# A grouped 3x3 convolution behind a group normalisation: the order of vector and scalar work between images, and 16-bit integers in the weights' quantisation

## The chip, the core and the metric

The kernel runs on one core of a Trainium2 chip. Five engines work side by side and wait for each other through semaphores: PE (TensorE, matmuls), DVE (VectorE), ACT (ScalarE), POOL (GpSimd) and SP (SyncE, which issues DMAs here). Each runs its instructions in the order in which the program hands them over. The metric is the time of one execution on the device, in microseconds (us); less is better.

## The reference, cut to what matters

The input x holds 160 images of 128 channels and 32 x 32 pixels. Each is normalised over groups of four channels. A 3x3 convolution with 128 output channels follows, with one of five weight sets for 32 images each, and the result is added to x. The weights are quantised in two steps by divisions rounded down:

```python
s1 = (jnp.max(U) - jnp.min(U)) / 3.0
v1 = s1 * floor(U / s1)
s2 = s1 / 5.0
v2 = s2 * floor((U - v1) / s2)
w = (v1 + v2).reshape(OUT_CH * N, IN_CH, 3, 3)      # N = 5 sets
act = conv(x_normalised, w, groups=5, padding=1)
return x + act
```

## The kernel before

**One image at a time.** An image is a tile of 128 channels by 1024 pixels. PE multiplies fp16 numbers, so the normalised image z (L491, ACT) is split in a high part hi (L499, ACT) and a rest lo (L548, DVE, `low_part`). Of the rest only sums and differences of rows are used (rows, L561 to L564, DVE, `combinations`). `conv` gives PE the products of an image: eo, and m for products with sums and differences of pairs of rows. m leaves PSUM by a copy on ACT (mm or mw, L672, `leave`), DVE makes pq of it (L684, L685, `pairs`) and adds eo to it (sum, L707 or L705, `residual`). POOL then issues a DMA that adds the sum to x in place (L720, `accumulate`), and SP stores the image.

**Combined images.** From image 14 on, every third image (i % 3 == 2) is a combined one: DVE forms row differences and sums v of x itself (L524, L527, L530, with two edges on POOL, L520 and L521, `combine`), ACT scales them to vh (L535), DVE makes the rest vl (L541, `low_combined`).

**Buffers.** eo has two buffers, so that conv of image i + 1 needs the sum of image i - 1. m has one, so that its next products need the copy of the last.

**Statistics.** The sum and sum of squares of an image come from two ACT passes (L192, L199, `measure` with stages 0 and 1), for some early images from DVE (L182 to L186; `by_vector` says which). For a group of eight images `means` is a small matmul over channels on PE (L208), `deviations` copies its result to ngm on ACT (L217) and forms dv on POOL (L219 to L222), `variances` is a second matmul (L225), `deviation` and `scales` make the factors: ve on ACT (L231), then rstd, shift and twice on POOL. Means and variances are placed after the first third of conv's products of an image and of the next one.

**Weights.** Set 0 is quantised at the start. Each other set is quantised while the set before it is in use, a column of the 3x3 window at a time: `make_column` is a generator of 14 DVE steps for a column (nearest integer L101, floor division L110 to L114, the rest L125, again, and L446). After them come three PE transposes (L451), two copies on ACT (wt, L456 and L457) and three operations on POOL (outer, L459, and wt, L460 and L461). From the fourth image of a set on, the loop takes two steps an image. The 15th step of a set falls to image 11 of it, the 29th to image 18, the end to image 25.

**The order.** It is written out by hand in `run`: an iteration hands over conv of image i, then statistics of images some 14 ahead, the copy of m, z and hi of image i + 3 or i + 4, DVE's work, deviations and factors, late statistics, the weight steps, and loads and stores.

Of the kernel before, what the change touches and what calls it, by code (L numbers as in the profile page):

```python
# [9 lines left out]
I32 = mybir.dt.int32  # L10
MM = mybir.dt.float16
ALU = mybir.AluOpType
# [4 lines left out]
N_SETS = 5  # L17
# [17 lines left out]
class Steps:  # L35
# [56 lines left out]
            nc.vector.scalar_tensor_tensor(far, self.s2, limit, far, op, ALU.max)  # L92
        nc.vector.tensor_copy(self.far, far)

    def nearest(self, pool, v, parts, name, by_scalar=False):

        tag = "ns" if by_scalar else "nn"
        dt = mybir.dt.int16 if by_scalar else I32
        n = pool.tile(list(v.shape), dt, tag=tag, name=f"{tag}_{name}")
        engine = self.nc.scalar.mul if by_scalar else self.nc.vector.tensor_scalar_mul  # L100
        engine(n, v, parts[0])  # L101
        return n

    def floor_div(self, k, v, n, t, parts):

        nc = self.nc
        r, _, hi, lo = parts
        yield nc.vector.scalar_tensor_tensor(t, n, hi, v, ALU.mult, ALU.add)  # L110
        yield nc.vector.scalar_tensor_tensor(t, n, lo, t, ALU.mult, ALU.add)
        yield nc.vector.scalar_tensor_tensor(t, t, r, n, ALU.mult, ALU.add)
        yield nc.vector.tensor_tensor(t, t, n, ALU.is_lt)
        yield nc.vector.tensor_sub(k, n, t)  # L114

    def quantise(self, pool, un, name, dt, by_scalar=False):


        yield (nn := self.nearest(pool, un, self.parts1, name, by_scalar))
        tt, k1, k2, rest = (  # L120
            pool.tile(list(un.shape), kind, tag=tag, name=f"{tag}_{name}")
            for tag, kind in (("tt", F32), ("k1", dt), ("k2", dt), ("rest", F32))
        )
        yield from self.floor_div(k1, un, nn, tt, self.parts1)
        yield self.nc.vector.scalar_tensor_tensor(  # L125
            rest, k1, self.parts1[1], un, ALU.mult, ALU.add
        )
        yield (nn := self.nearest(pool, rest, self.parts2, name + "_2"))
        yield from self.floor_div(k2, rest, nn, tt, self.parts2)
        return k1, k2  # L130


def run(steps):

    while True:
        try:
            next(steps)
        except StopIteration as end:
            return end.value
# [169 lines left out]
class Main:  # L309
# [153 lines left out]


    def by_vector(self, i):
        return self.EARLY <= i < self.EARLY + 18 and i % 2 == 0

    def measure(self, i, stages=(0, 1)):

# [259 lines left out]
    def run(self):  # L729
        nc, P = self.nc, self.P  # L730
# [3 lines left out]
        for n in range(N_SETS):  # L734
            if n == 0:
                un = self.upool.tile([P, P, TAPS], F32, tag="u", name="u0")
# [32 lines left out]
        def take(steps, count):  # L769
            for _ in range(count):  # L770
                next(steps, None)
# [71 lines left out]
        for i in range(self.imgs):  # L843
            n, b = self.place(i)
# [29 lines left out]
                and k - 3 - (self.combined(k - 1) and self.group_of[k] == self.group_of[k - 1])  # L874
                == i
            ]
            if self.combined(i + 1):
                self.low_combined(i + 1)
            if self.combined(i + 2):
                self.combine(i + 2)  # L880

            stages = (0, 1) if self.combined(i - 1) else (0,)
            for k in to_measure:
                if not self.by_vector(k):
                    self.measure(k, stages)
            if i >= self.FIRST and not self.combined(i):
                self.leave(i)
            for k in parted:
                self.normalise(k)
            if self.combined(i):  # L890
                self.leave(i)
            for k in parted:
                self.high_part(k)
            if self.combined(i + 2):
                self.high_combined(i + 2)
            if i + 2 < self.STEADY:
                if self.FIRST < i + 2:
                    self.low_part(i + 2)
                    self.combinations(i + 2)
            if i > self.FIRST:  # L900
                self.residual(i - 1)
                self.accumulate(i - 1)

            if i >= self.FIRST and not self.combined(i):
                self.pairs(i)
            if self.STEADY <= i + 2 < self.imgs and not self.combined(i + 2):
                self.low_part(i + 2)
                self.combinations(i + 2)
            if self.combined(i):
                self.pairs(i)  # L910
            for st in middle:
                st.deviation()
                st.scales()
            for st in ready:
                st.deviations()
            middle, ready = ready, []
            for k in to_measure:
                if self.by_vector(k) or 1 not in stages:
                    self.measure(k, (1,))
                group = self.group_of[k]  # L920
                if k + 1 == self.groups[group].stop:
                    ready.append(self.stats[group])
            if b == self.per_set // 16 and n + 1 < N_SETS:
                self.load_set(n + 1)
            if b == self.per_set // 8 and n + 1 < N_SETS:
                later = (s for col in self.COLS for s in self.make_column(n + 1, col))
            if later is not None:
                take(later, 2)
                if b == self.per_set - 1:
                    run(later)  # L930
            self.store(i - 2)
            while loaded * NB < min(self.imgs, i + self.LOAD_LEAD):
                self.load(loaded)
# [50 lines left out]
```

## Time and profile before

| what | us |
|---|---|
| median of three runs | 1059.19 |
| lowest and highest | 1054.25, 1059.98 |
| profiled execution, as timed | 1059.3 |
| span of its instructions | 1057.4 |
| ACT busy | 845.8 (80%) |
| POOL busy | 400.7 (38%) |

The profiled execution was taken at a mean PE clock of 0.992. Its page gives each engine's busy time. PE's busy time says little by itself, since matmuls overlap: one of 496 columns counts as 0.38 us and the next one starts about 0.216 us later. Where PE shows idle time, it waited for something. The view of waits says for what, and the windows give the same numbers for stretches of the span. These are DVE's quantisation steps in it, each of 384 elements a partition:

```profile
L113 DVE TENSOR_TENSOR tt<-tt,nn 128x384 f32<-128x384 f32 x28 | 15.5, 555 | 0.5
L114 DVE TENSOR_TENSOR k<-nn,tt 128x384 f16<-128x384 int32 x28 | 15.5, 555 | 0.7
L446 DVE SCALAR_TENSOR_TENSOR m<-k,k 128x384 f16<-128x384 f16 x12 | 6.7, 558 | 0.4
```

The columns are line, engine, operation, output and inputs, shapes and count, then the time of all in us, the mean of one in ns, and the engine's idle time before them.

### The profile page before, as it was taken

How to read it: one execution, taken by the hardware profiler on the slowest of the kernel's cores; microseconds unless marked ns; L12 is line 12 of the kernel's file. 1: busy time of each engine (PE TensorE's matmuls, PEld its weight loads, DVE VectorE, ACT ScalarE, POOL GpSimd, SP SyncE). 2: the span in 40 equal slices, each digit the busy share in tenths (PEclk: the TensorE clock that was granted, in tenths of full speed). 3: DMA queues.
4: the chain of work that ended last, by engine and by line, in shares of the span. 5: the costliest groups of instructions: out<-in, count | busy, mean ns of one | idle time of the engine just before them, and what ended most of it. 6: DMA issues, size and time to landing. Idle time of an engine off the chain costs nothing.

```text
span 1057.4 us, 15888 instructions
## 1 busy us (share of the span) xinstructions
PE 1000.4 (95%) x5910; PEld 578.2 (55%) x5910; DVE 970.3 (92%) x1399; ACT 845.8 (80%) x1113; POOL 400.7 (38%) x517
## 2 busy tenths in 40 slices
PE   1899998999999999999999999999989999999997
PEld 0355554555565555656555555555545556565554
DVE  7999999998999999989999988899999988888975
ACT  4787696898888978988887879888969988886551
POOL 4432426272325253442445262525242623333410
PEclk9999998999999999999999999999999999999999
DMA  9548988899998998999899898998989999988673
GB/s 362 209 132 207 239 239 239 229 243 263 280 264 255 236 253 224 272 279 270 247 244 250 235 284 240 274 241 240 247 233 249 256 275 263 260 213 213 159 179 123
DMA packets 67286, 254.42 MB, mean 241 GB/s; under 512 B 5248, under 2 KB 5248, under 8 KB 67200
## 3 DMA queue, kind: packets, MB, share of 16 engines
q1 hardware_dynamic: 45168, 173.09, 47.8%
q0 software_dynamic: 22032, 80.23, 39.3%
q8 instruction: 48, 0.79, 0.3%
q14 instruction: 38, 0.31, 0.1%
HBM read 89.19 MB, written 83.89 MB: 164 GB/s over the span
## 4 chain that ended last, share of the span: by engine, by line
PE 44%; DVE 40%; issue 7%; POOL 5%; ACT 3%; DMA 1%; SPq 0%; POOLq 0%; DVEq 0%; ACTq 0%
PE eo L588 20%; PE m L624 12%; PE eo L624 11%; DVE sum L707 5%; DVE lo L548 5%; DVE vl L541 4%; DVE rows L561 3%; DVE v L524 2%; DVE sum L705 2%; DVE rows L563 2%; DVE rows L564 2%; DVE pq L684 1%; DVE pq L685 1%; DVE v L527 1%; ACT vh L535 1%
## 5 line engine op out<-in xcount | busy, mean ns | idle before, releaser
L588 PE MATMUL eo<-hi,wt 128*128 128x496 f16 (+3 forms) x1998 | 483.7, 379 | 4.5 <-DVE sum L705 2.4
L624 PEld LDWEIGHTS <-wt 128*128 128x128 f16 x3690 | 361.7, 99 | 218.2 <-issue 3.3
L720 POOL DMA_DIRECT2D xt<-sum x153 | 134.6, 880 | 547.6 <-DVE sum L707 291.4
L588 PEld LDWEIGHTS <-wt 128*128 128x128 f16 x2070 | 204.1, 99 | 202.7 <-issue 12.7
L624 PE MATMUL eo<-rows,wt 128*128 128x248 f16 (+1 forms) x1308 | 198.1, 274 | 0.0
L199 ACT ACTIVATE junk<-xt,mv 128x1024 f16<-128x1024 f32 x151 | 173.2, 1147 | 1.6
L192 ACT ACTIVATE junk<-xt 128x1024 f16<-128x1024 f32 x151 | 159.1, 1054 | 13.7 <-DMA xt<-in_x_dram 10.9
L672 ACT ACTIVATE mm<-m 128x1024 f16<-128x1024 f32 x109 | 110.8, 1017 | 66.2 <-PE m L624 64.9
L624 PE MATMUL m<-rows,wt 128*128 128x496 f16 (+1 forms) x654 | 159.1, 379 | 0.8 <-ACT mm L672 0.6
L541 DVE SCALAR_TENSOR_TENSOR vl<-v,rstd,vh 128x2048 f16<-128x2048 f32 x48 | 112.8, 2349 | 34.0 <-ACT vh L535 34.0
L491 ACT ACTIVATE z<-xt,shift,rstd 128x1024 f32<-128x1024 f32 x112 | 137.8, 1230 | 5.3 <-POOL shift L241 5.3
L548 DVE TENSOR_TENSOR lo<-z,hi 128x1024 f16<-128x1024 f32 x112 | 137.0, 1223 | 0.0
L535 ACT ACTIVATE vh<-v,rstd 128x2048 f16<-128x2048 f32 x48 | 95.9, 1999 | 50.8 <-DVE v L530 36.4
L707 DVE SCALAR_TENSOR_TENSOR sum<-pq,eo 128x1024 f32<-128x1024 f16 x105 | 127.6, 1215 | 7.6 <-PE eo L624 7.6
L499 ACT CAST hi<-z 128x1024 f16<-128x1024 f32 x112 | 116.7, 1042 | 2.2
L624 PE MATMUL eo<-vl,wt 128*128 128x248 f16 (+1 forms) x576 | 110.2, 273 | 0.0
L624 PE MATMUL eo<-vh,wt 128*128 128x248 f16 (+1 forms) x576 | 110.1, 273 | 0.0
L624 PE MATMUL m<-vl,wt 128*128 128x496 f16 (+1 forms) x288 | 109.3, 380 | 0.0
L624 PE MATMUL m<-vh,wt 128*128 128x496 f16 (+1 forms) x288 | 109.3, 380 | 0.0
L672 ACT ACTIVATE mw<-m 128x1024 f32<-128x1024 f32 x48 | 48.7, 1015 | 48.7 <-PE m L624 48.6
L561 DVE TENSOR_TENSOR rows<-lo 128x1024 f16<-128x1024 f16 x109 | 75.9, 696 | 3.7
L684 DVE TENSOR_TENSOR pq<-mm 128x512 f16<-128x512 f16 x109 | 45.9, 421 | 18.8 <-ACT mm L672 18.8
(114 smaller groups left out, 990.2 us busy)
## 6 DMA issues: line engine op xcount, KB each, us to landing
xt<-in_x_dram SPq DMA_DIRECT2D x78, 1024.0 KB, 9.4
out_dram<-xt SPq DMA_DIRECT2D x78, 1024.0 KB, 5.5
xt<-sum POOLq DMA_DIRECT2D x153, 512.0 KB, 6.8
range<-in_L_conv_U_dram SPq DMA_DIRECT2D x4, 576.0 KB, 7.1
u<-in_L_conv_U_dram SPq DMA_DIRECT2D x4, 576.0 KB, 12.1
xt<-in_x_dram SPq DMA_DIRECT2D x4, 512.0 KB, 9.3
out_dram<-xt SPq DMA_DIRECT2D x3, 512.0 KB, 2.8
u<-in_L_conv_U_dram SPq DMA_DIRECT2D x2, 288.0 KB, 2.9
```

Source lines behind the costliest of these rows:

```text
L192: self.nc.scalar.activation(junk, image, ACTF.Copy, scale=-1.0 / image.shape[1], accum_out=self.mv[:, j, 0:1],)
L199: self.nc.scalar.activation(junk, image, ACTF.Square, bias=self.mv[:, j, 0:1], accum_out=self.mv[:, j, 1:2],)
L491: nc.scalar.activation(z, self.image(i), ACTF.Identity, bias=st.shift[:, j : j + 1], scale=st.rstd[:, j : j + 1],)
L499: self.nc.scalar.copy(hi.rearrange("p h w -> p (h w)"), self.z[i])
L541: self.nc.vector.scalar_tensor_tensor(vl, self.v[i], st.rstd[:, j], self.hi[i], ALU.mult, ALU.subtract)
L548: self.nc.vector.tensor_sub(lo[:, 1 : self.H + 1, :].rearrange("p h w -> p (h w)"), self.z.pop(i), self.hi[i].rearrange("p h w -> p (h w)"),)
L561: nc.vector.tensor_sub(d, lo[:, 0:H, :], lo[:, 2 : H + 2, :])
L588: nc.tensor.matmul(target[:, h, r0 - h0 : r1 - h0, c0:c1], self.wts[n, col][:, k, :], tile[:, s0 : s0 + r1 - r0, c0 + dw : c1 + dw], start ...
L624: nc.tensor.matmul(target[:, :, c0:c1], self.wts[n, col][:, kind, :], source[:, :, c0 + dw : c1 + dw], start=start, stop=stop,)
L672: self.nc.scalar.mul(m, self.m.pop(i).rearrange("p a i w -> p a (i w)"), scale)
L707: nc.vector.scalar_tensor_tensor(self.sum[i], self.m.pop(i), 0.5 / UP, eo, ALU.mult, ALU.add)
L720: self.nc.gpsimd.dma_start(self.image(i), self.sum.pop(i), accum_op=ALU.add)
```

## The change

In the quantisation the nearest integers become int16 and the result of the comparison becomes fp16 (`below`), so that the last subtraction has 16-bit operands alone. In the loop DVE's and ACT's operations are put in another order, in which one that reads a result seldom follows the one that wrote it; the weight steps move from the end of the iteration to places before and after `pairs`, ahead of the deviations; and fewer images have their statistics from DVE (four in place of nine).

```diff
-    def nearest(self, pool, v, parts, name, by_scalar=False):
+    def nearest(self, pool, v, parts, name, dt, by_scalar=False):
...
-        yield nc.vector.tensor_tensor(t, t, n, ALU.is_lt)
-        yield nc.vector.tensor_sub(k, n, t)
+        yield nc.vector.tensor_tensor(below, t, n, ALU.is_lt)
+        yield nc.vector.tensor_sub(k, n, below)
...
+        ints = mybir.dt.int16 if dt == MM else I32
+        yield (nn := self.nearest(pool, un, self.parts1, name, ints, by_scalar))
...
+        below = pool.tile(list(un.shape), MM, tag="lt", name=f"lt_{name}") if dt == MM else tt
...
-        return self.EARLY <= i < self.EARLY + 18 and i % 2 == 0
+        return self.EARLY <= i < self.EARLY + 8 and i % 2 == 0
...
-            if self.combined(i + 1):
-                self.low_combined(i + 1)
-            if self.combined(i + 2):
-                self.combine(i + 2)
-
-            stages = (0, 1) if self.combined(i - 1) else (0,)
-            for k in to_measure:
-                if not self.by_vector(k):
-                    self.measure(k, stages)
+            if b == self.per_set // 16 and n + 1 < N_SETS:
+                self.load_set(n + 1)
+            if b == self.per_set // 8 and n + 1 < N_SETS:
+                later = (s for col in self.COLS for s in self.make_column(n + 1, col))
+            by_scalar = [k for k in to_measure if not self.by_vector(k)]
+            for k in by_scalar:
+                self.measure(k, (0,))
+            if self.combined(i - 1):
+                for k in by_scalar:
+                    self.measure(k, (1,))
             if i >= self.FIRST and not self.combined(i):
                 self.leave(i)
             for k in parted:
                 self.normalise(k)
             if self.combined(i):
                 self.leave(i)
+            elif not self.combined(i - 1):
+                for k in by_scalar:
+                    self.measure(k, (1,))
             for k in parted:
                 self.high_part(k)
+            low = i + 2 if self.FIRST < i + 2 < self.imgs and not self.combined(i + 2) else None
+            if self.combined(i + 1):
+                self.low_combined(i + 1)
             if self.combined(i + 2):
+                self.combine(i + 2)
                 self.high_combined(i + 2)
-            if i + 2 < self.STEADY:
-                if self.FIRST < i + 2:
-                    self.low_part(i + 2)
-                    self.combinations(i + 2)
+            if low is not None:
+                self.low_part(low)
             if i > self.FIRST:
                 self.residual(i - 1)
                 self.accumulate(i - 1)
-            if i >= self.FIRST and not self.combined(i):
+            if low is not None:
+                self.combinations(low)
+            if later is not None:
+                take(later, 1)
+            if i >= self.FIRST:
                 self.pairs(i)
-            if self.STEADY <= i + 2 < self.imgs and not self.combined(i + 2):
-                self.low_part(i + 2)
-                self.combinations(i + 2)
-            if self.combined(i):
-                self.pairs(i)
+            if later is not None:
+                take(later, 1)
+                if b == self.per_set - 1:
+                    run(later)
             for st in middle:
                 st.deviation()
                 st.scales()
             for st in ready:
                 st.deviations()
             middle, ready = ready, []
+            if self.combined(i):
+                for k in by_scalar:
+                    self.measure(k, (1,))
             for k in to_measure:
-                if self.by_vector(k) or 1 not in stages:
-                    self.measure(k, (1,))
+                if self.by_vector(k):
+                    self.measure(k)
...
-            if b == self.per_set // 16 and n + 1 < N_SETS:
-                self.load_set(n + 1)
-            if b == self.per_set // 8 and n + 1 < N_SETS:
-                later = (s for col in self.COLS for s in self.make_column(n + 1, col))
-            if later is not None:
-                take(later, 2)
-                if b == self.per_set - 1:
-                    run(later)
```

The order in which PE and SP get their instructions is the same before and after.

More of the change, by code (lines that the diff above doesn't have):

```diff
@@ L93, in choose @@
         nc.vector.tensor_copy(self.far, far)
-    def nearest(self, pool, v, parts, name, by_scalar=False):
+    def nearest(self, pool, v, parts, name, dt, by_scalar=False):
         tag = "ns" if by_scalar else "nn"
-        dt = mybir.dt.int16 if by_scalar else I32
         n = pool.tile(list(v.shape), dt, tag=tag, name=f"{tag}_{name}")
@@ L102, in nearest, with floor_div @@
         return n
-    def floor_div(self, k, v, n, t, parts):
+    def floor_div(self, k, v, n, t, below, parts):
         nc = self.nc
@@ L112, in floor_div @@
         yield nc.vector.scalar_tensor_tensor(t, t, r, n, ALU.mult, ALU.add)
-        yield nc.vector.tensor_tensor(t, t, n, ALU.is_lt)
-        yield nc.vector.tensor_sub(k, n, t)
+        yield nc.vector.tensor_tensor(below, t, n, ALU.is_lt)
+        yield nc.vector.tensor_sub(k, n, below)
     def quantise(self, pool, un, name, dt, by_scalar=False):
-        yield (nn := self.nearest(pool, un, self.parts1, name, by_scalar))
+        ints = mybir.dt.int16 if dt == MM else I32
+        yield (nn := self.nearest(pool, un, self.parts1, name, ints, by_scalar))
         tt, k1, k2, rest = (
@@ L123, in quantise @@
         )
-        yield from self.floor_div(k1, un, nn, tt, self.parts1)
+        below = pool.tile(list(un.shape), MM, tag="lt", name=f"lt_{name}") if dt == MM else tt
+        yield from self.floor_div(k1, un, nn, tt, below, self.parts1)
         yield self.nc.vector.scalar_tensor_tensor(
@@ L127, in quantise @@
         )
-        yield (nn := self.nearest(pool, rest, self.parts2, name + "_2"))
-        yield from self.floor_div(k2, rest, nn, tt, self.parts2)
+        yield (nn := self.nearest(pool, rest, self.parts2, name + "_2", ints))
+        yield from self.floor_div(k2, rest, nn, tt, below, self.parts2)
         return k1, k2
```

## The prediction

> **What bounds the kernel now.** I read the page's busy line first, then the waits, then the timeline round the waits, then windows with and without weight work. Images go in threes: a combined one (i % 3 == 2, from 14 on), the one after it (0) and the one before the next (1).
>
> ```profile
> PE 1000.4 (95%) x5910; PEld 578.2 (55%) x5910; DVE 970.3 (92%) x1399; ACT 845.8 (80%) x1113; POOL 400.7 (38%) x517
> ...
> PE pg L225 <- POOL dv L222: 24.9, 14, 4.9
> PE eo L588 <- DVE sum L705: 2.4, 6, 0.5
> ...
> 530.63:602.87 72.24, 70.65 (x424) 41.05 (x422) 71.55 (x105) 60.64 (x82) 29.46 (x38) 1.00 0.91 240
> 837.30:909.54 72.24, 72.24 (x436) 42.34 (x434) 63.23 (x85) 64.10 (x83) 22.56 (x31) 1.00 0.98 269
> ...
> 153.00:178.00 25.00, 22.26 (x120) 12.27 (x118) 23.03 (x34) 18.57 (x28) 14.18 (x16) 0.86 0.89 237
> 605.00:629.00 24.00, 21.56 (x124) 12.24 (x122) 21.33 (x31) 19.34 (x29) 13.92 (x18) 0.93 0.99 279
> 757.00:782.00 25.00, 21.75 (x123) 12.24 (x122) 24.50 (x37) 19.56 (x29) 13.04 (x17) 0.93 0.92 232
> ```
>
> In the windows the columns are length, then busy time of PE, PEld, DVE, ACT and POOL, then PE's clock. TensorE is the bound: without weight steps (837 to 910) it has no idle time and three images take 18.06 us, DVE working 15.8 of them. With two weight steps an image (531 to 603) DVE is full (71.55 of 72.24; in the timeline its rounds, from one L524 to the next combined image's, take about 19.05 us, as from 558.91 to 578.00) and PE idles 1.6 us. So what a faster DVE can win is PE's idle time alone. By window minus PE busy it is: 2.74 in 153 to 178, 2.61 in 306 to 378, 0.67 in 378 to 419, 1.33 in 492 to 547, 1.59 in 547 to 605, 2.44 in 605 to 629, 0.83 in 701 to 757, 3.25 in 757 to 782. The three low clocks cost another 25 x 0.14 = 3.5, 24 x 0.07 = 1.7 and 25 x 0.07 = 1.8 us. Most of the idle time is the wait of the variance matmul (L225) for POOL's dv: behind lagging DVE work, in iterations of kind 0, because ngm stands behind vh, which waits for v (L530).
>
> ```profile
> 549.17 1.22 DVE L548 TENSOR_TENSOR lo<-z,hi 128x1024 f16<-128x1024 f32 x1
> 550.42 0.69 DVE L561 TENSOR_TENSOR rows<-lo 128x1024 f16<-128x1024 f16 x1
> 551.03 0.42 DVE L563 TENSOR_TENSOR rows<-lo 128x512 f16<-128x512 f16 x1
> ...
> 367.10 0.16 ACT L217 COPY ngm<-pg 128x8 f32<-128x8 f32 x1
> ...
> 368.30 0.48 ACT L456 ACTIVATE wt<-pt 128x384 f16<-128x384 f32 x1
> ...
> 367.31 0.33 PE L451 MATMUL pt<-ident,m 128*128 128x128 f16 x3
> ...
> 370.60 0.39 PE L225 MATMUL pg<-dv,gavg 128*128 128x8 f32 x2 [1.26 <-POOL dv L222]
> ...
> 368.44 0.81 POOL L219 TENSOR_TENSOR dv<-mv,ngm 128x8 f32<-128x8 f32 x1
> ...
> 370.51 0.87 POOL L459 TENSOR_TENSOR outer<-wt 128x128 f16<-128x128 f16 x1
> ```
>
> Two things to see. L561 reads what L548 wrote and starts 0.03 us after its end; L563 does not read L561 and starts 0.08 before its end. A dependent pair costs 0.117 us more on DVE. And at image 50 the order is ngm, weight copy on ACT, and dv, then outer on POOL; this order is what the change turns round.
>
> [...] 1024 elements took 0.696 us in f16 (L561), 1.223 with f32 inputs (L548). [...] L220 took 2.20 us at 168.1, beside a vl (L541) of 2.3 us, against a median of 0.59. [...] The three windows above have waits of 2.4 to 3.3 us and clocks of 0.86 to 0.93; waits of 1.3 show none.
>
> **The change part by part.**
> - DVE, gaps. low_part, sum and the row differences now stand apart, and one weight step stands before the pairs, one after them. Per three images this takes away two dependent pairs of L548/L561 and three of weight steps: 5 x 0.117 = 0.59 us.
> - DVE, 16 bits. L114 has int16 and f16 alone now: from 0.555 to about (half of 1024's slope) 0.36, so 0.2 less, twice in 14 steps; six steps per three images: 0.17 us. L113 still reads an f32: 0 (bounds 0 and -0.2). L101 to int16: 0, bounds -0.1 and +0.1. The STT steps show no gain from 16 bits (L446, all f16: 0.558).
> - Together a loaded round comes to 19.05 - 0.59 - 0.17 = 18.3 us, against PE's 18.06 to 18.55 (transposes included). DVE stops falling behind. What goes: eo waits in 378 to 419 (+0.65), 547 to 605 (+1.6) and 701 to 757 (+0.8); the wait at image 90 with its clock (2.44 + 1.7: +4.1), at image 42 (+1.3), half of that at image 74 (1.33 to 0.6: +0.7). At 66 and 138, the same place without weight work, PE waits under 0.1, which is why I take 42 and 90 whole. Late next is PE itself.
> - low_part before sum delays the eo bank's release by 1.13 us at most. Without load the sum ends 3.8 us or more before PE needs the bank, and for kind 2 it waits for PE anyway: cost 0; bounds 0 and +1.
> - Start: the chain of the first two columns holds four L114; PE waits 1.51 us for the second at 40.3. +0.8.
> - Five images (16 to 24, even) go from DVE's statistics (two L182 of 0.68, with the rest about 1.7) to ACT (L192 and L199 with their reads, 2.2 from start to start). In windows of 13 us from 73 to 125 DVE is full (12.7) and ACT has 2.5 to 5.6 us free; with the five ACT needs about 6.3 us an image (copy, z and hi 3.0, 1.5 statistics of 2.2), PE 6.42. Cost 0, bounds 0 and +2.
> - The second statistic now stands before hi and ngm in kind 1 and the early images: ngm is 1.2 us later less 0.4 of gaps. At image 3, where ACT is full and PE already waits 1.47 us, -0.5. Elsewhere 1.0 to 3.5 us of slack cover it.
> - The weight steps move ahead of the deviations, with all they issue: PE's transposes (same place in PE's order), two wt copies on ACT, three wt operations on POOL. Where a column ends in the same iteration as a group's deviations (images 11, 18, 50, 82, 114), ngm now waits on ACT behind the wt copies, which wait for PE's transposes after the whole conv; and dv waits on POOL behind outer and two wt operations. On ACT the next statistic and, an iteration later, the next copy of m are queued behind; that copy has 2 to 3 us of slack. With Te the transposes' end: copies end at Te + 0.8; the three POOL operations took 1.3 to 3.4, median 2.05; dv's four 1.6 to 3.7, 3.2 to 3.7 beside vl (kind 0). PE wants dv at Te + 3.0 (11, 18, 114), + 1.6 (50), + 3.3 (82).
>  - Image 50: dv at Te + 0.8 + 2.05 + 2.4 = 5.3, stall 3.7 and about 2 of clock, for 1.26 now: -4.5.
>  - Image 82: dv (here 2.0) at 4.9, stall 1.6, for none: -1.8 with a chance of clock.
>  - Image 11: ACT-bound no more but Te-bound; 2.5 to 2.7 for 2.14 now, and half a chance of clock: -1.0.
>  - Images 18 and 114: v is no longer late, but dv at Te + 6.0 gives a stall of 3.0, as now (2.74 and 2.93): 0 and, with an eo wait gone, +0.5.
>  - At 43, 75 and 107 it is ve, not ngm, that comes behind the weight operations: shift is about 2 us later; the z that needs it comes 8 us later at 43 and 107, and at 75 ACT waits 2 us of some 3 that the copy of m has: 0, bounds 0 and +1.
> - load_set stands earlier in the source, but SP's order of DMAs is the same, and so is PE's: 0.
>
> Sum: 0.65 + 1.6 + 0.8 + 4.1 + 1.3 + 0.7 + 0.8 - 0.5 - 4.5 - 1.8 - 1.0 + 0.5 = 2.65 us. The profiled execution took 1059.3 (span 1057.4), the same as the median of 1059.19 (1054.25 to 1059.98). Forecast: 1056.6, no change that can be told.
>
> **Rivals.**
> - The relief wins (faster). If POOL's operations keep their short durations where vl is not beside them (1.3 + 1.6), dv comes at Te + 3.7: stall 2.0 without clock at 50 (+3.8 against the forecast), none at 82 (+1.8), 0.7 at 11 (+2.4): 1048.6. For it: a less crowded DVE blocks POOL less. Against: the medians.
> - The collisions win (slower). One mechanism: dv behind the weight operations at those five images, at the upper durations (2.8 + 3.2): dv at Te + 6.8; stalls with clock lose 3.5, 1.1, 6.8, 3.4 and 1.3, 16.1 in all, where the forecast has 6.8 net: 1065.9. It decides once dv ends past about Te + 6.5 in all five. For it: 15 wt triples hold four over 2.7, and each stall past 2.4 costs clock too. Against: all five at the upper end is rare.
> - The change does not do what it says: rounds stay near 19 us, because something other than the pair's gap fills the time. The gains of 9.2 fall away: 1065.8. Against: 226 dependent pairs have gaps near 0.034 and 549 independent ones -0.083.
>
> **How the numbers follow.** Forecast 0.55 (own range 1051 to 1062), relief 0.22, collisions 0.18, no effect 0.05. Over 0.5% is 5.3 us, about what can be told from no change: under 1053.9 is faster, over 1064.5 slower. Faster: 0.9 of the relief and 0.18 of the forecast, 0.30. Slower: 0.7 of the last two and a little of the forecast, 0.18. Same 0.52. Range 1047 to 1066.
>
> **What would show it.** Right: L114 at 0.36 and L113 near 0.55; L561 no more behind L548; DVE rounds of about 18.3 in loaded stretches, no PE wait for sums; L225 waits of 3 to 4 us at image 50 and 1 to 2 at 82, with outer just before dv; no wait at image 90. Wrong: L225 waits under 1 us at 18, 50 and 114 (then faster), new waits for mm or mw copies between 60 and 130 (ACT over-full), or PE waiting for sums more than now.

## The result and the profile after

| | before | after |
|---|---|---|
| median of four runs, us | 1058.74 | 1072.37 |
| lowest and highest, us | 1054.25, 1059.98 | 1071.05, 1074.63 |
| profiled execution, span, us | 1057.4 | 1069.0 |

The ratio is 1.0133, with a 95% interval of 1.010 to 1.0167: the change makes the kernel slower by 1.3%, 13.6 us, where 1056.6 and a range of 1047 to 1066 had been forecast.

From L126 on, line numbers of the changed kernel are one higher than before: L226 is the variance matmul, L220 to L223 are dv, L460 to L462 outer and wt on POOL, L521 and L522 the edge rows of v. In the floor division they are one lower (L112 compares, L113 subtracts). The busy line of its page:

```profile
PE 1002.5 (94%) x5910; PEld 579.4 (54%) x5910; DVE 938.5 (88%) x1374; ACT 849.0 (79%) x1133; POOL 447.9 (42%) x517
```

DVE has 32 us less to do, ACT 3 more, and POOL, with the same 517 instructions, 47 more. The waits (us in total, times, longest):

```profile
PE pg L226 <- POOL dv L223: 38.0, 17, 4.9
...
POOL outer L460 <- ACT wt L457: 33.2, 11, 6.8
...
PE eo L589 <- DVE sum L708: 1.8, 2, 1.6
```

PE waits less for sums (3.2 before, 1.8 now), as forecast, and 13 us more for dv. The groups by form show what became of single operations (busy us, mean ns, idle before); first before the change, then after it:

```profile
L520 POOL TENSOR_SCALAR v<-xt,ngm 128x32 f32<-128x32 f32 x48 | 51.2, 1067 | 1.5
L219 POOL TENSOR_TENSOR dv<-mv,ngm 128x8 f32<-128x8 f32 x18 | 17.1, 949 | 8.9 <-ACT ngm L217 8.9
...
L459 POOL TENSOR_TENSOR outer<-wt 128x128 f16<-128x128 f16 x15 | 10.9, 724 | 13.7 <-ACT wt L456 13.6
```

```profile
L521 POOL TENSOR_SCALAR v<-xt,ngm 128x32 f32<-128x32 f32 x48 | 92.6, 1929 | 1.5
...
L220 POOL TENSOR_TENSOR dv<-mv,ngm 128x8 f32<-128x8 f32 x18 | 26.4, 1467 | 9.5 <-ACT ngm L218 9.5
...
L460 POOL TENSOR_TENSOR outer<-wt 128x128 f16<-128x128 f16 x15 | 22.5, 1500 | 33.2 <-ACT wt L457 33.2
...
L113 DVE TENSOR_TENSOR k<-nn,lt 128x384 f16<-128x384 int16 x28 | 9.8, 351 | 0.2
```

DVE's L113 fell from 555 to 351 ns. On POOL the same operations on the same 32, 8 and 128 elements a partition went from 1067, 949 and 724 ns to 1929, 1467 and 1500. The windows round the worst waits, and one without weight steps (length, busy PE, PEld, DVE, ACT, POOL, then PE's clock):

```profile
151.00:177.00 26.00, 21.29 (x118) 11.89 (x116) 22.13 (x35) 17.48 (x26) 17.50 (x18) 0.87 0.84 217
362.00:387.00 25.00, 20.34 (x117) 11.49 (x115) 21.68 (x34) 17.54 (x26) 14.55 (x18) 0.93 0.84 232
515.00:540.00 25.00, 20.66 (x119) 11.50 (x117) 21.71 (x35) 17.10 (x26) 12.79 (x15) 0.93 0.82 232
764.00:791.00 27.00, 21.91 (x118) 12.14 (x117) 23.04 (x36) 18.33 (x27) 17.75 (x18) 0.87 0.92 246
865.50:901.90 36.40, 36.40 (x223) 21.45 (x221) 31.26 (x43) 31.80 (x43) 12.56 (x19) 1.00 0.95 260
```

In the first four PE idles 4 to 5 us and then runs at a lowered clock; they hold images 18, 50, 74 and 114. Over the whole trace from 45 us on, the gaps between matmuls add up to 33.1 us, against 22.1 before; the waits of L226 among them grew by 13 (17.8 to 31.2), the rest fell by 2. The lowered clock is a granted share of 0.5 in the trace's clock records, for 3.4 or 6.8 us at a time; counted at half their length, these stretches cost 10.2 us here from 45 us on, and 6.8 before. Image 18 in the timeline (start, us, engine), first the two lines of before that show dv ahead of outer, then after:

```profile
168.10 2.20 POOL L220 TENSOR_SCALAR dv<-dv 128x8 f32<-128x8 f32 x1
...
170.82 0.42 POOL L459 TENSOR_TENSOR outer<-wt 128x128 f16<-128x128 f16 x1
```

```profile
164.36 2.34 DVE L542 SCALAR_TENSOR_TENSOR vl<-v,rstd,vh 128x2048 f16<-128x2048 f32 x1
164.39 0.16 ACT L218 COPY ngm<-pg 128x8 f32<-128x8 f32 x1
164.42 3.70 POOL L460 TENSOR_TENSOR outer<-wt 128x128 f16<-128x128 f16 x1 [0.53 <-ACT wt L457]
...
166.62 1.22 DVE L549 TENSOR_TENSOR lo<-z,hi 128x1024 f16<-128x1024 f32 x1
...
167.75 1.21 DVE L708 SCALAR_TENSOR_TENSOR sum<-pq,eo 128x1024 f32<-128x1024 f16 x1
168.20 0.43 POOL L461 TENSOR_TENSOR wt<-outer,wt 128x128 f16<-128x128 f16 x1
...
168.97 0.67 POOL L220 TENSOR_TENSOR dv<-mv,ngm 128x8 f32<-128x8 f32 x1
...
170.89 0.60 PE L226 MATMUL pg<-dv,gavg 128*128 128x8 f32 x2 [4.71 <-POOL dv L223]
```

Two things meet here. Outer now stands ahead of dv, though ngm is ready at 164.55. And outer lasts 3.70 us, against 0.42 before: it comes to an end only after vl and lo, which now stand back to back, when DVE has gone on to the sum, one of whose inputs is in PSUM. ACT is late here too: vh, which stands ahead of the column's copies, had waited 1.30 us for POOL's edge rows, of which the first took 4.52 us. At image 74 no weight column ends, and dv itself is what lasts. Before:

```profile
516.93 0.82 POOL L219 TENSOR_TENSOR dv<-mv,ngm 128x8 f32<-128x8 f32 x1
517.01 0.69 DVE L561 TENSOR_TENSOR rows<-lo 128x1024 f16<-128x1024 f16 x1
...
519.09 0.39 PE L225 MATMUL pg<-dv,gavg 128*128 128x8 f32 x2 [1.33 <-POOL dv L222]
```

and after:

```profile
521.81 3.26 POOL L220 TENSOR_TENSOR dv<-mv,ngm 128x8 f32<-128x8 f32 x1
...
522.78 0.69 DVE L686 TENSOR_TENSOR pqw<-mw 128x512 f32<-128x512 f32 x1
523.38 0.55 DVE L447 SCALAR_TENSOR_TENSOR m<-k,k 128x384 f16<-128x384 f16 x1
...
523.85 1.15 DVE L525 TENSOR_TENSOR v<-xt 128x960 f32<-128x960 f32 x1
...
525.16 1.20 POOL L221 TENSOR_SCALAR dv<-dv 128x8 f32<-128x8 f32 x1
...
526.98 0.39 PE L226 MATMUL pg<-dv,gavg 128*128 128x8 f32 x2 [4.34 <-POOL dv L223]
```

From the trace alone two theories stand. Q: the queue order is the loss (weight operations ahead of ngm on ACT and of dv on POOL). A: DVE's new order blocks POOL. A third, O, would put it down to ACT's order and load.

### The profile page after: what moved, and what is told of

Same layout as the page of the kernel before. It is cut to its first block, busy times and chain, and to the rows that moved or that the text cites. A ratio compares the mean times of both kernels' runs of the same rounds, so it can differ in the third digit from the quotient of the medians.

```text
span 1069.0 us, 15887 instructions
## 1 busy us (share of the span) xinstructions
PE 1002.5 (94%) x5910; PEld 579.4 (54%) x5910; DVE 938.5 (88%) x1374; ACT 849.0 (79%) x1133; POOL 447.9 (42%) x517
## 5 line engine op out<-in xcount | busy, mean ns | idle before, releaser
L200 ACT ACTIVATE junk<-xt,mv 128x1024 f16<-128x1024 f32 x156 | 178.6, 1145 | 1.7
L193 ACT ACTIVATE junk<-xt 128x1024 f16<-128x1024 f32 x156 | 164.5, 1054 | 12.1 <-DMA xt<-in_x_dram 10.5
L521 POOL TENSOR_SCALAR v<-xt,ngm 128x32 f32<-128x32 f32 x48 | 92.6, 1929 | 1.5
```

Of the source, the lines that this page charges most:

```text
L193: self.nc.scalar.activation(junk, image, ACTF.Copy, scale=-1.0 / image.shape[1], accum_out=self.mv[:, j, 0:1],)
L200: self.nc.scalar.activation(junk, image, ACTF.Square, bias=self.mv[:, j, 0:1], accum_out=self.mv[:, j, 1:2],)
```

## The experiments

All times are medians. In this section "before" was measured beside every set of runs, at 1057.5 to 1059.2 us. The ratios are not the quotients of these medians, and effects read from them differ from those read from the medians by up to some 4 us; where it matters both are given. How long dv lasts is the sum of its four operations.

**How long POOL waits beside DVE.** A kernel for this alone (`m_block`): in each stretch DVE repeats one form, its outputs in two tiles in turn, and POOL runs ten small operations.

```diff
+        elif name == "f32":
+            v.tensor_sub(t[:, :512], a[:, :512], b[:, :512])
+        elif name == "f32dep":
+            v.tensor_sub(t[:, :512], to[:, :512], b[:, :512])
...
+            g_.tensor_scalar_mul(m8, e8, 0.5)
+            g_.tensor_tensor(m8, m8, e8, ALU.mult)
```

> Leaves out the whole computation: fourteen stretches of about 16 us in which VectorE runs one form of instruction back to back while POOL runs its small operations (128x8, 128x32, 128x128). Theory A (VectorE blocks POOL through the two SBUF inputs of its instructions): beside an idle VectorE POOL's 128x8 operations take 0.2 to 0.3 us; beside lo (f32 and f16 inputs), vl and the f32 pair forms back to back each takes more than 1 us or ends only with VectorE's stretch; beside the sums, which read one input from PSUM, under 0.6 us. Theory A' (it is the gap between dependent instructions that lets POOL in): the dependent f32 and f16 forms give under half of the time of the independent ones of the same form. Theory B (POOL is slow for another reason, such as its own queue): the same 0.2 to 0.5 us in all stretches.

| DVE's form, back to back | one of DVE's, start to start, us | POOL's 128x8 operations, us |
|---|---|---|
| idle | | 0.19 to 0.23 |
| lo, 1024 elements | 1.17 | 1.02 to 1.20 |
| vl, 2048 elements | 2.30 | 2.15 to 2.32 |
| sums, one input in PSUM | 1.14 | 0.19 to 0.23 |
| f32 pairs of 512, independent | 0.61 | 16.23 (the first; the others after the end) |
| f32 pairs of 512, dependent | 0.74 | 0.23 to 0.67 |

The timeline of the f32 pairs:

```profile
41.36 16.23 POOL L74 TENSOR_TENSOR p<-e,tok 128x8 f32<-128x8 f32 x1 [5.79 <-DVE tok L72]
57.56 0.23 POOL L81 TENSOR_SCALAR m<-e 128x8 f32<-128x8 f32 x1
57.87 0.20 POOL L82 TENSOR_TENSOR m<-m,e 128x8 f32<-128x8 f32 x1
```

Theory B falls. Beside lo and vl back to back POOL's operations ended one to a border of DVE's: 1.02 to 1.20 us each beside lo, whose borders lie 1.17 us apart, and 2.15 to 2.32 beside vl, with 2.30. Beside independent f32 pairs one missed all 26 borders (16.23 us). Theory A' fits the f32 pairs alone: beside f16 pairs of 512 elements POOL's 128x8 operations took 0.22 to 0.40 us where DVE's instructions were independent and 0.21 to 0.40 where they were dependent. At one to a border a chain of seven operations (outer, two wt, four dv) would take seven of DVE's instructions, an estimate from these times.

**Undoing parts of the change.** Four kernels are the changed one but for one part. In `u_ends` the columns' ends (transposes, copies and POOL's three operations) stand behind the deviations again, while the steps on DVE stay where they are:

```diff
             parts = ((m, self.ident),)
-        pt = self.ps_tr.tile([P, ROW, P], F32, tag="pt", name=f"pt{n}_{col}")
+            self.ends.append(lambda: self.end_column(n, col, parts))
+            return
...
             middle, ready = ready, []
+            for end in self.ends:
+                end()
+            self.ends.clear()
```

> The changed kernel with the ends of the weight columns (transposes, their two copies on ACT, three operations on POOL) put behind the deviations again; the steps on VectorE stay where the change put them. Theory Q (queue order: ngm and dv stand behind the weight operations): the stalls of the variance matmul at images 18, 50, 82 and 114 (4.7, 4.7, 1.3, 4.9 us) fall to about 2.7, 1.3, 0 and 2.9 as before the change, and with the clock the time falls by 10 to 14 us to 1058 to 1062; image 74 keeps its 4.3. Theory A alone (POOL is blocked by VectorE wherever its operations stand): dv keeps 3 to 5 us, the stalls stay over 3.5 at 18 and 114, the time at 1067 or more.

In `u_low` low_part stands behind the sum and, with it, the row differences behind the pairs:

```diff
-            if low is not None:
-                self.low_part(low)
             if i > self.FIRST:
                 self.residual(i - 1)
                 self.accumulate(i - 1)
             if low is not None:
-                self.combinations(low)
+                self.low_part(low)
...
                 self.pairs(i)
+            if low is not None:
+                self.combinations(low)
```

> The changed kernel with low_part again behind the sum, one weight step and the pairs between it and the row differences. Theory A: vl (2.3 us) and lo (1.2 us) no longer stand back to back, POOL's outer at images 18 and 114 falls from 3.7 to about 2.4 us and the mean of POOL's edge rows from 1.9 to about 1.2; the stalls at 18 and 114 fall from 4.8 to about 3.5, that at 74 to about 1.5; the time falls by 6 to 10 us to 1062 to 1066. Theory Q alone: the order on ACT and POOL is the same, the time stays within 3 us of 1072.

In `u_act` the second statistic stands behind the deviations, in `u_vec` DVE has its nine images of statistics:

```diff
-            elif not self.combined(i - 1):
-                for k in by_scalar:
-                    self.measure(k, (1,))
...
-            if self.combined(i):
+            if not self.combined(i - 1):
                 for k in by_scalar:
```

```diff
-        return self.EARLY <= i < self.EARLY + 8 and i % 2 == 0
+        return self.EARLY <= i < self.EARLY + 18 and i % 2 == 0
```

> The changed kernel with the second statistic behind the deviations again in kind 1 and the early images. By the prediction this order costs 0.5 us at image 3 (stall 1.94 back to about 1.5) and nothing elsewhere: 1070 to 1074. Theory O (order on ACT is the loss): the stalls at 26, 42, 122 fall and the time with them by 4 us or more.

> The changed kernel with by_vector over 18 images again, five more statistics on VectorE. By the prediction ACT's extra load costs nothing between images 3 and 24 (bounds 0 and +2): 1070 to 1074. Theory L (ACT's load is the loss): the time falls by 4 us or more, all of it before 130 us.

| kernel | us | ratio to before, 95% |
|---|---|---|
| u_ends | 1062.43 | 1.0045 (1.0032 to 1.0058) |
| u_low | 1064.73 | 1.0078 (1.0052 to 1.0104) |
| u_act | 1073.43 | 1.0149 (1.0119 to 1.018) |
| u_vec | 1073.44 | 1.0142 (1.0112 to 1.0173) |

ACT's order and load cost nothing, and theory O falls. The queue order takes 10 us, low_part's place with that of the row differences 7.6 (9.3 and 5.8 by the ratios). In `u_ends` the stalls at 18, 82 and 114 went as theory Q has it, but that at 50 stayed at 4.1 in place of 1.3: dv, no longer behind outer, lasts 4.8 us there. In `u_low` outer at image 18 came to an end with vl, after 2.42 us; but image 74, for which a stall of 1.5 had been expected, kept 4.5, and dv took 6.0. POOL's edge rows kept a mean of 1.84 us (the first of each pair), where 1.2 had been expected, and the stall at 114 rose to 5.4.

**Which half of the queue order, and do the two losses add?** In `u_pool` only POOL's three weight operations go behind dv; `u_ends_low` has both diffs, of `u_ends` and `u_low`.

```diff
+        self.wts[n, col] = wt
+        if n > 0:
+            self.ends.append(lambda: self.add_taps(n, col, wt))
+            return
...
+    def add_taps(self, n, col, wt):
```

> The changed kernel with POOL's three weight operations alone put behind dv; PE's transposes and ACT's copies stay ahead of ngm. If the POOL part of the collision is most of it: dv starts with ngm at 164.4 beside vl and ends near 168.4, the stalls at 18 and 114 fall from 4.8 to about 2.4, at 50 from 4.7 to about 3.8 (dv is then blocked itself, as in the kernel with the whole ends behind), at 82 to about 0.5; 1062 to 1067. If it is ACT's copies ahead of ngm: stalls within 0.5 of the changed kernel, 1071 or more.

> The changed kernel with the columns' ends behind the deviations and low_part behind the sum. Alone they took 10.0 and 7.6 us away. If they are two separate losses: 1053 to 1057. If they are the same loss seen twice (weight operations ahead of dv, made long by vl and lo): 1059 to 1062.

`u_pool` took 1063.57, 8.8 us less than the changed kernel, so nearly all of the queue order's loss is on POOL. `u_ends_low` took 1052.45, 0.9936 of before (0.9919 to 0.9953): 19.9 us less than the changed kernel, 2.3 more than both alone. They are two losses.

**Parts of the change alone, on the kernel before.** `p_16` has the change's `nearest`, `floor_div` and `quantise` and nothing else of it. `p_early` has besides `take(later, 2)` ahead of the deviations; DVE's order stays. `p_low` has besides the 16 bits low_part ahead of the sum.

```diff
                 self.pairs(i)
+            if later is not None:
+                take(later, 2)
...
             for st in ready:
                 st.deviations()
...
-                take(later, 2)
```

```diff
+            if self.STEADY <= i + 2 < self.imgs and not self.combined(i + 2):
+                self.low_part(i + 2)
             if i > self.FIRST:
                 self.residual(i - 1)
...
-                self.low_part(i + 2)
                 self.combinations(i + 2)
```

> The kernel before with the 16 bit integers and comparisons alone. By the prediction L114 falls from 0.555 to 0.36 us in six steps of three images, 0.17 us of 19 in loaded rounds: 0 to 3 us less, 1055.5 to 1059. If a VectorE with less time per round is in itself harmful (theory A: it comes to lie differently against POOL), the time rises by 2 us or more.

> The kernel before with 16 bits, and the two weight steps with all they issue ahead of the deviations; VectorE's order is that of before. Theory Q (the queue order costs by itself): stalls of 4 us or more at 18, 50 and 114, as after the change, and with the clock 1059 to 1063, against 1051.0. Theory A (it is VectorE's new order that makes these operations long): POOL's weight operations and dv keep the durations of before, stalls of 3 to 3.7, 1053 to 1057.

> The kernel before with 16 bits and low_part alone put ahead of the sum; the rest in the order of before. If lo directly behind vl costs through POOL whatever else is changed: dv at images 26, 42, 66, 90, 122 takes 0.8 us more, stalls there rise by as much, and the time goes from 1051.0 to 1056 to 1060. If it costs only with the weight operations ahead: 1050 to 1053. If it is the eo bank, released later: PE waits for sums (now 2 to 3 us in all) rise by 4 us or more, without longer dv.

| kernel | us | ratio to before, 95% |
|---|---|---|
| p_16 | 1050.97 | 0.9947 (0.9928 to 0.9966) |
| p_early | 1065.31 | 1.0065 (1.0053 to 1.0078) |
| p_low | 1060.91 | 1.0032 (1.002 to 1.0044) |

The 16 bits alone win 7 us (5.6 by the ratio), more than expected. The queue order alone costs 14.3 us on top of them (12.5), so it costs in DVE's old order too. The time is above what either theory expected, while the stalls at 18, 50 and 114 (3.3, 3.7 and 4.3 us) lie between the two. The profiled executions differ by 13.4 us, of which 7.7 is idle time; the rest goes with PE's halved clock, counted at 8.5 us here and at none in `p_16`. low_part alone costs 9.9 (9.0). In the profiled executions, 8.7 us apart, 4.4 us of it are longer waits for dv and 3.4 the halved clock. dv lasts longer: at images 42, 66 and 90 it took 3.8 to 3.9 us instead of 2.9 to 3.1, at 26 and 122 3.1 instead of 1.9, while PE's waits for sums rose by 1.2 us in all. At 50 and 74 dv also starts 0.5 and 0.8 us later after the mean matmul: the DMA that adds the sum to x stands ahead of dv on POOL and waits for the later sum. Here are the stalls of L226 (idle time of PE ahead of it, us) and the idle time of PE from 45 us on:

| image | before | after | u_ends | u_low | u_ends_low | p_16 | p_early | p_low |
|---|---|---|---|---|---|---|---|---|
| 11 | 2.1 | 2.0 | 0 | 1.1 | 0 | 1.8 | 3.3 | 1.8 |
| 18 | 2.7 | 4.7 | 2.6 | 3.3 | 1.8 | 2.5 | 3.3 | 2.6 |
| 42 | 1.4 | 1.1 | 1.1 | 0.3 | 0.3 | 1.0 | 0.9 | 1.3 |
| 50 | 1.3 | 4.7 | 4.1 | 5.2 | 4.3 | 1.0 | 3.7 | 1.8 |
| 74 | 1.3 | 4.3 | 4.3 | 4.5 | 4.5 | 1.2 | 1.2 | 1.5 |
| 82 | 0 | 1.3 | 0 | 1.8 | 0 | 0 | 1.2 | 0 |
| 90 | 2.4 | 1.8 | 1.9 | 0.9 | 0.9 | 2.4 | 2.4 | 2.5 |
| 114 | 2.9 | 4.9 | 2.6 | 5.4 | 2.9 | 2.9 | 4.3 | 2.6 |
| 122 | 0.7 | 1.1 | 1.1 | 0 | 0 | 0.6 | 1.1 | 1.4 |
| all idle | 22.1 | 33.1 | 25.9 | 25.2 | 16.9 | 19.2 | 26.9 | 24.9 |

**The sum between the pairs and v.** What is left in `u_ends_low` are images 50 and 74. A way to break DVE's run there is to put the sum of the combined image ahead of the next v (`residual` before `combine`); `e_sumv` is the changed kernel with this, `u_three` has it together with the two moves above.

```diff
             if i > self.FIRST:
                 self.residual(i - 1)
+            if self.combined(i + 2):
+                self.combine(i + 2)
+                self.high_combined(i + 2)
+            if i > self.FIRST:
                 self.accumulate(i - 1)
```

> The changed kernel with the sum of a combined image (one input from PSUM) put between its pairs and the next combined image's v, which are all of two SBUF inputs. Theory A (POOL waits through VectorE's run of such instructions): at image 74 dv's first operation, 3.26 us, ends with m before the sum, the four take under 3 us instead of 4.9 and the stall falls from 4.3 to about 2.3; at image 50 from 4.7 to about 3.5; with the clock the time falls by 3 to 7 us, 1065 to 1069. In the other direction vh comes 1.1 us later on ACT, with ngm behind it at images 18, 90 and 114. Theory Q alone: no stall at 74 changes, 1072 to 1075.

> The changed kernel with three moves at once: the columns' ends behind the deviations, low_part behind the sum, the sum ahead of the next v. If queue order and blocked POOL operations are the whole loss, and the two add: stalls of about 2.7 at 18 and 114, 1.5 at 50, 2.3 at 74, none at 82, and 1051 to 1056, as fast as the kernel before with 16 bits alone or nearly. If something else in the change costs (ACT's load, its order), it stays at 1058 or more.

This missed: 1077.71 (ratio 1.0188, 1.0155 to 1.0221) and 1064.94 (1.0052, 1.0036 to 1.0068). The stalls at 74 and 50 in `e_sumv` fell to 2.3 and 3.4 as theory A has it, but v and with it vh and ngm come later: the stall at 42 rose from 1.1 to 3.2, at 90 from 1.8 to 2.3. In `u_three` those at 18, 42, 50, 74, 90 and 114 are all 2.6 to 3.4. So putting an operation with an input in PSUM into the run freed dv and lost more elsewhere.

**Breaking DVE's runs.** Five memsets of one column (0.06 us each; the expectations say six) for each combined image: behind vl, between the two pairs, and ahead of each of v's three operations. `e_gaps` is the changed kernel with them, `u_best` is `u_ends_low` with them, `p_gaps` is `p_16` with them. `u_rows` is `u_ends_low` without memsets, but with the row differences ahead of the pairs in a combined image's iteration.

```diff
+    def gap(self):
+        self.nc.vector.memset(self.pause, 0.0)
...
         nc.vector.tensor_add(rows[:, :, 0], m[:, 0], m[:, 1])
+        if self.combined(i):
+            self.gap()
         nc.vector.tensor_sub(rows[:, :, 1], m[:, 0], m[:, 1])
```

```diff
+            if low is not None and self.combined(i):
+                self.combinations(low)
             if i >= self.FIRST:
                 self.pairs(i)
-            if low is not None:
+            if low is not None and not self.combined(i):
                 self.combinations(low)
```

> The changed kernel with six one-column memsets on VectorE per combined image (about 0.06 to 0.1 us each), behind vl, between the pairs of a combined image and ahead of and between the three operations of v; nothing else moves. Theory A (POOL gets in only where VectorE's run of two-input instructions is broken): dv at image 74 falls from 4.86 to under 3 us and the stall from 4.3 to about 2; the mean of POOL's first edge row falls from 1.93 to 1.2 or less; the stalls at 18 and 114 fall to about 3.5 since outer ends with vl; 1060 to 1067. If a broken run doesn't let POOL in: the same durations, 1072 to 1075.

> The changed kernel with the columns' ends behind the deviations, low_part behind the sum, and the six one-column memsets. Without the memsets it took 1052.5, with stalls of 4.3 and 4.5 us at images 50 and 74 where dv took 6.0. If POOL's blocked operations are what costs there: dv about 3, stalls of about 2 and 2.5, and with the clock 1045 to 1050. If they are not: 1052 to 1055.

> The kernel before with 16 bits and the six memsets. In that order POOL's operations are short already (edge rows 1.06 us, dv under 3.5): 1048 to 1053, no gain over 1051.0 that can be told, or up to 3 us if the blocked operations at images 18, 90 and 114 get shorter.

> The same as the one before without memsets, but in the iteration of a combined image the row differences stand ahead of the pairs, so that dv meets operations of f16 as before the change and not the run of f32 pairs and v. If this is why dv takes 6.0 us at images 50 and 74: about 2 there, stalls of 1 to 2, 1044 to 1049. If dv's place against DVE is not the cause: 1052 to 1055.

| kernel | us | ratio to before, 95% |
|---|---|---|
| e_gaps | 1074.23 | 1.0143 (1.0128 to 1.0159) |
| p_gaps | 1052.89 | 0.9967 (0.9951 to 0.9982) |
| u_rows | 1051.97 | 0.9955 (0.9941 to 0.997) |
| u_best | 1036.67 | 0.9826 (0.98 to 0.9853) |

`u_best` is the fastest of all and faster than expected, 1.7% under the kernel before by the ratio and 14 us under `p_16` by the medians: PE's idle time is 8.8 us, no stall after 45 us is over 2.2. In `e_gaps` POOL's operations became short as expected (edge rows 1.10 us, dv at 74 3.0, stall 2.5), but the time did not fall: at 18 and 114 the seven operations still have to pass vl and lo (stalls of 4.2), at 50 it is 4.8. So blocked operations cost where they stand on PE's path, and with the weight operations ahead of dv the path stays too long. In `p_gaps` there was little to win, and it is 1.9 us slower than `p_16`. Image 74 in the timeline (line numbers are those of each kernel), in `u_ends_low`, which differs from `u_best` by the memsets alone:

```profile
514.28 0.36 DVE L113 TENSOR_TENSOR k<-nn,lt 128x384 f16<-128x384 int16 x1
514.33 4.39 POOL L220 TENSOR_TENSOR dv<-mv,ngm 128x8 f32<-128x8 f32 x1
```

in `u_rows`:

```profile
508.10 0.35 DVE L113 TENSOR_TENSOR k<-nn,lt 128x384 f16<-128x384 int16 x1
508.14 4.39 POOL L220 TENSOR_TENSOR dv<-mv,ngm 128x8 f32<-128x8 f32 x1
...
509.64 0.68 DVE L692 TENSOR_TENSOR pqw<-mw 128x512 f32<-128x512 f32 x1
...
512.38 0.75 DVE L535 SCALAR_TENSOR_TENSOR v<-xt,twice 128x512 f32<-128x512 f32 x1
```

and in `u_best`:

```profile
503.80 0.35 DVE L113 TENSOR_TENSOR k<-nn,lt 128x384 f16<-128x384 int16 x1
503.84 0.98 POOL L220 TENSOR_TENSOR dv<-mv,ngm 128x8 f32<-128x8 f32 x1
...
504.68 0.69 DVE L702 TENSOR_TENSOR pqw<-mw 128x512 f32<-128x512 f32 x1
504.70 0.06 DVE L580 MEMSET pause<- 128x1 f32 x1
504.91 0.55 POOL L221 TENSOR_SCALAR dv<-dv 128x8 f32<-128x8 f32 x1
```

dv meets the same instruction k at the same point. Without a break its first operation waits, in both orders, through k, the three f16 row differences, two f32 pairs, m and the first part of v (6.0 us for its four operations); with the memset between the pairs its first operation is over at 504.82, and all four take 2.3. That f16 differences would let it in, the expectation of `u_rows`, was wrong.

**Which borders are open?** A second kernel for this alone, `m_open`, with forms in turn:

```diff
+    plan = [("f32",), ("f32long",), ("f32short",), ("stt",), ("k",),
+            ("f32", "mem"), ("f32", "stt"), ("f32", "nn"), ("f32", "sumtt"),
...
+            ("k", "f32", "mem", "f32", "f16", "f16short", "f16short")]
```

> Leaves out the whole computation: fifteen stretches of about 10 us of VectorE's forms alone and in turn, with POOL's small operations beside each. If only the form counts: f32 pairs never open (each POOL operation ends with the stretch), in any length, and one open form between them (STT, one input, PSUM, f16) lets POOL in once a turn, as a memset does. If it is the border's kind (the same operation following itself stays shut): the turns of two operations all open, and f32 alone and k alone stay shut. If it is the time between borders: f32 of 384, 512 and 1024 elements differ. The last two stretches repeat the order of images 50 and 74 without and with a memset between the pairs: shut for 3 us or more without, open within 1.3 us with it.

None of these: here f32 pairs of 384, 512 and 1024 elements all let POOL in at each border (its 128x8 operations took 0.49 to 0.67 us beside 512, the form that had kept it out for 16.23), and k (f16 from int16) kept it out for all 36 instructions:

```profile
65.36 9.75 DVE L70 TENSOR_TENSOR s<-q,g 128x384 f16<-128x384 int16 x36
65.53 9.65 POOL L89 TENSOR_TENSOR p<-e,tok 128x8 f32<-128x8 f32 x1 [4.75 <-DVE tok L87]
```

All turns of two forms were open, and so were the last two stretches; but in those some operations that follow each other wrote the same tile and stood apart by a gap, so that they don't repeat images 50 and 74. What decides whether an unbroken run lets POOL in stays open; the form alone does not. Where POOL got in, DVE had an input in PSUM (the sums of `m_block`: 0.19 to 0.23 us), a gap (its dependent f32 pairs, 0.74 us from start to start in place of 0.61: 0.23 to 0.67) or a memset (`u_best`: dv's first operation ended at 504.82, the memset at 504.76), but also plain borders: those of lo and vl in `m_block` and of the f32 pairs in `m_open`.

## Why the prediction was wrong

**Right.** L113 at 0.351 us (forecast 0.36) and the comparison unchanged at 0.551; DVE's loaded rounds, from one L525 to the next, took 18.1 to 18.4 us where PE did not stall (forecast 18.3; since PE's own pace is 18.06, this shows only that DVE kept up); PE's waits for sums went down; ACT's five statistics cost nothing (`u_vec`), nor did ACT's order at more than image 3, where the stall is 1.9 us and 1.2 without it (`u_act`); the mechanism of the collisions at 18, 50, 82 and 114, outer just ahead of dv; and image 82 (forecast 1.6, 1.3 measured). The stall at image 11 was 2.0, under the forecast 2.5 to 2.7.

**"low_part before sum ... cost 0; bounds 0 and +1".** This step was furthest off: 7.6 to 10 us in three comparisons (`u_low` against after, `u_ends_low` against `u_ends`, `p_low` against `p_16`), of which only the last moves low_part alone. I priced the path that the code names, the release of the eo bank, and that was nearly free (PE's waits for sums rose by 1.2 us in `p_low`). The loss came by a path that no semaphore shows: lo stands directly behind vl, and POOL's next operation waited for both: at image 18 outer took 3.70 us beside vl (2.34) and lo (1.22), against 0.42 before, and in `u_low`, with lo further back, 2.42. The prediction had such waits in its durations, but only for dv beside vl. `m_block` has them for one instruction (2.15 to 2.32 us beside vl of 2.30) and, where instructions stand back to back, for many: 16.23 us across 27 f32 pairs.

**The collisions' sizes.** With Te the end of PE's transposes (163.18 at image 18), "the three POOL operations took ... median 2.05" was the term that was too small: they took 4.6 us at 18 (164.42 to 169.02) and 4.6 at 114. The copies came to an end at Te + 1.3, not + 0.8, since ACT was still at vh, which had waited for the edge rows. dv's own four took 1.9 of the 3.2 allowed. So dv was there at Te + 7.7 in place of + 6.0, and the stall 4.7, not 3.0 (4.9 at 114); "0 and, with an eo wait gone, +0.5" became some 2 us of idle time each. At 50 it was Te + 6.3 for 5.3, and 4.7 for 3.7. Queue order alone cost 14.3 us (`p_early`), where the five collisions had been put at 6.8 net. A median over all 15 columns was the wrong number for 18 and 114, whose operations stand beside vl and lo; at 11 and 82 they took 2.0 and 2.2, near the median.

**Image 74.** Forecast as a gain of 0.7, it became a stall of 4.3. dv starts about as long after the mean matmul as before (3.1 and 3.0 us), but DVE is 1.2 us further on, and dv meets k, the pairs and v without a break instead of the row differences behind lo. A faster and denser DVE was only counted as relief. That 15.8 us (11.6 by the ratios) hang on waits of this kind and the clock that they cost, once the queue order is undone, is what `u_best` against `u_ends_low` shows. Which part of the new order leaves the run at 74 unbroken was not taken apart: it stays in `u_ends`, `u_low` and `u_rows`.

**The gains.** "The wait at image 90 with its clock (2.44 + 1.7: +4.1)" came to 0.7 of idle time and the clock, and that at image 42 (+1.3) to 0.3. The 16 bits, put at 0.17 us a round, won 7 us alone (5.6 by the ratio, 3.6 to 7.6 by its interval); their profiled execution shows 2.9 us less idle time and no low clock from 45 us on, where the kernel before lost 6.8 us by it (window by window of 12 us, length times one less the clock). The clock's share is not a sure gain, as the last section shows.

**The rivals.** The collisions' rival had the right mechanism, and its price of 1065.9 is close to that of queue order alone; what it left out is low_part. The relief's rival needed short POOL operations. "A less crowded DVE blocks POOL less" did not show: with the 16 bits alone the first edge rows kept their 1.06 us (`p_16`; 1.07 before), and in the changed kernel, where DVE has less to do but fewer breaks, they took 1.93.

## What to carry to other kernels

When operations of VectorE are moved next to each other, look at what POOL does at that time and who waits for it: here the order that suited VectorE took more from PE, by way of POOL, than VectorE had to give (VectorE's busy time fell by 32 us, PE's idle time rose from 22.1 to 33.1). Before moving a step ahead of another, take the durations that its operations have in that very place, not their median, and count the whole chain that stands on a queue. Where the path of the bound engine goes over POOL, a broken run on VectorE can be worth far more than it costs: memsets of 0.06 us won 15.8 us in `u_best`. They won nothing in `e_gaps`, where POOL's queue was too long, nor in `p_gaps`, where the run was not in the way, and moving the sum into the run lost (`e_sumv`, `u_three`).

## What the hardware showed that I had not expected

An unbroken run of two-input operations on VectorE kept a POOL operation of 0.2 us waiting for up to 16.23 us, over 26 borders (`m_block`), and at another time the same form let it in at each (0.49 to 0.67 us, `m_open`). In `u_low` an edge row of 32 elements took 5.65 us (L521 at 765.82).

PE's clock does not follow from a stall's length alone. In the clock records of the seventeen whole kernels, from 45 us on, PE ran at half rate 70 times, for 3.4 or 6.8 us, each time beside a stall. None of the 81 stalls of 0.7 to 1.7 us had such a stretch, 38 of the 67 of 1.75 to 3.34 us did, and all 32 from 3.36 us on. Before the change the three stretches stand beside the stalls of 2.74, 2.44 and 2.93 us at images 18, 90 and 114, after it the four beside those of 4.71, 4.66, 4.34 and 4.91 at 18, 50, 74 and 114. The same stall of 2.93 us at image 114 lowered the clock before the change (0.93 in 757 to 782 us) and not in `p_16`, as its timeline and window show:

```profile
767.42 0.39 PE L226 MATMUL pg<-dv,gavg 128*128 128x8 f32 x2 [2.93 <-POOL dv L223]
```

```profile
749.00:775.00 26.00, 22.88 (x142) 13.34 (x140) 25.73 (x39) 19.94 (x30) 14.24 (x19) 1.00 0.96 256
```

So the prediction's "each stall past 2.4 costs clock too", read from three stalls, does not hold. A stretch of 3.4 us costs about 1.7 us, an estimate from its length at half rate; what decides whether a stall of 1.75 to 3.34 us has one beside it, no run shows. The prediction's "waits of 2.4 to 3.3" hold one sum of idle time in place of a wait: the longest wait in the three windows was 2.93.
